# A two-layer graph network on one core: leaks taken from PSUM in groups of eight pairs, terms made a batch ahead

## The chip, the cores and the metric

The kernel runs on one core of a Trainium2 chip. A core has TensorE (PE, matrix products; PEld is its loading of weights), VectorE (DVE), ScalarE (ACT), GpSimd (POOL) and SyncE (SP). Each takes its instructions in order from its own queue, and semaphores join them. SP, ACT and POOL also start DMA transfers. SBUF is the working memory of 128 partitions, PSUM the smaller memory that TensorE writes into, in banks of 2 KB a partition, which is 512 numbers of four bytes. The metric is the time of one execution on the device in microseconds (us).

## The reference, cut to what matters

There are 12,500 nodes with 64 features and 400,000 edges, which are sorted by their target. The first layer computes a message per edge and sums the messages by target:

```
x_i, x_j = x[dst], x[src]
h = leaky_relu(concat([x_i, x_j - x_i]) @ W1 + b1, 0.01)
h = leaky_relu(h @ W2 + b2, 0.01)
x = layernorm(x + segment_sum(h, dst))
```

The second layer is an attention over the same edges and one loop per node, with four heads: logits `a_src[src] + a_dst[dst]`, a leak of 0.2, a softmax over the edges of a target, a weighted sum of the sources' features, the mean over the heads, and again a layernorm of the sum.

## The kernel before, in words

The first product is split: `x_i @ (W1a - W1b) + b1` belongs to the target and `x_j @ W1b` to the source, so both are computed once per node, and an edge needs one addition only. The nodes are ranked by their number of edges and cut into 98 windows of 128, one node to a partition. Window `w` has `KW[w]` edge slots, 64 in the first, 46 in the second, down to 19 in the last, 3180 in all. The kernel has three stages.

**Preparation** (L461 to L697). Nodes lie in 98 columns of 128. The columns go in eight batches: six of 14, then 8, then 6. For each batch POOL fetches a row of edge data per column (`gather_rows` into `rt`, L585). The class `Terms` makes the two products of four columns: `turn` transposes on TensorE and copies to `xt` on ACT; `multiply` forms `pab` on TensorE, then VectorE adds `b1` into `rt` (L499) and ACT copies twice into `bt` (L503, L504). The class `Bins` counts nodes by degree, four columns at a time: `mark` makes the one-hot `oh` on VectorE (L517), three sorts of small products on TensorE (L522, L526, L529) and a copy on ACT; `place` multiplies and reduces on VectorE (L535, L537). `in_step` sets the order of these in every queue: the terms of batch `k` go with the bins of batch `k - 1`. Behind each pass come `lt` and its reduction (L590, L593), which need the fetched rows of batch `k`, and from them the degrees, which the next bins need. SP writes `rt` and `info` to the table `xtab` and loads the node features of batch `k + 2` into one of three buffers `rt`. After the last pass the ranks follow (L610 to L697), and `bt` is written to the tables `btab`.

**First layer** (L834 to L990). `load_rows` fetches the rows of several windows from `xtab`, and `index_slots` turns them into indices on VectorE (`make_slots`, L253 to L265, and `mask_slots`). `fetch0(w)` lets POOL gather a row of 128 nodes for each slot, two slots side by side as a pair, into `g`, which has five buffers (`gp`). It is called two windows ahead. Pairs are worked on in groups of up to four: `expand` transposes each pair into PSUM (L878) and VectorE adds the target's term on the way to SBUF (L880); `leak` multiplies by 0.01 and takes the maximum, in place in SBUF (L884); `second` is the second product (L889), brought to SBUF by ACT with the bias (L891), and a leak again; `collect` sums over the pairs by a product with `both`, which TensorE accumulates in PSUM (L898), and VectorE reduces that at the window's end (L903). `norm` adds the node's own features, takes the layernorm and, from `g`, writes the sources' ranks over the indices; `logits` makes the attention terms and SP writes the rows to `t1tab` and `state`. The loop at L968 is an order written out by hand: in step `i` the second product of group `i - 2`, the expansion of group `i`, the collection of group `i - 4`, with norm and logits one and two steps behind. A window's groups come last pairs first, so that a window starts when most of its rows are there.

**Second layer** (L1058 to L1226). POOL gathers rows of `t1tab` for the same 3180 slots; VectorE weighs and reduces them (L1129, L1136). It needs the whole of `t1tab`, so that its first gather waits for the last window of the first layer.

Of the kernel before, what the change touches and what calls it, by code (L numbers as in the profile page):

```python
# [21 lines left out]
P = 128  # L22
# [40 lines left out]
def tile_gnn_resnorm(ctx: ExitStack, tc: tile.TileContext, x, src, dst, w1, b1, w2, b2,  # L63
# [397 lines left out]
    with tc.tile_pool(name="prep", bufs=1) as prep, \  # L461
            tc.tile_pool(name="prep2", bufs=2) as prep2, \
            tc.tile_pool(name="prep3", bufs=3) as prep3, \
# [17 lines left out]
        class Terms:  # L481
# [12 lines left out]
            def multiply(self):  # L494
                n, g0, g1 = self.n, self.g0, self.g1
                pab = pps2.tile([P, 4, 2 * D], F32, name="pab")
                for w in range(n):
                    nc.tensor.matmul(pab[:, w, :], self.xt[:, w, :], wab, start=True, stop=True)
                nc.vector.tensor_tensor(  # L499
# [39 lines left out]
        def load_inputs(b0, b1_):  # L539

            n = b1_ - b0
            rt = prep3.tile([P, DW, X0 + ER], F32, name="rt")
# [4 lines left out]
            for l0, l1 in ((0, cut), (cut, NFULL)):  # L547
                if l0 < l1:
                    nc.sync.dma_start(
                        rt[l0:l1, :n, :D],  # L550
                        x[l0 * NW:l1 * NW, :].rearrange("(p w) d -> p w d", w=NW)[:, b0:b1_, :])
            if b0 < NREST:
                c1 = min(b1_, NREST)
                nc.sync.dma_start(
# [4 lines left out]
        def degrees(a, b):  # L559
            nc.vector.tensor_sub(deg[:, a:b], ptr[:, a + 1:b + 1], ptr[:, a:b])  # L560
            nc.scalar.copy(info[:, a:b, 1], deg[:, a:b])
            nc.scalar.copy(info[:, a:b, 2], ptr[:, a:b])
            nc.sync.dma_start(xtab_v[:, a:b, XL:], info[:, a:b, :])
            return [Bins(g, min(g + 4, b)) for g in range(a, b, 4)]

        def in_step(terms, bins):
            for i in range(max(len(terms), len(bins)) + 1):
                if i < len(terms):
# [3 lines left out]
                if i < len(terms):  # L572
                    terms[i].multiply()
                if 0 <= i - 1 < len(bins):
                    bins[i - 1].place()

        rts = [load_inputs(*batches[0]), load_inputs(*batches[1])]
        nc.vector.tensor_sub(wab[:, :D], w1a, wab[:, D:])
        bins = []
        sorted_to = 0  # L580
        for k, (b0, b1_) in enumerate(batches):
# [4 lines left out]
            in_step([Terms(rt, b0, g, min(g + 4, b1_)) for g in range(b0, b1_, 4)], bins)  # L586
# [17 lines left out]
            if k + 2 < len(batches):  # L604
                rts.append(load_inputs(*batches[k + 2]))
# [95 lines left out]
    with tc.tile_pool(name="l0", bufs=1) as l0:  # L701
# [132 lines left out]
        with tc.tile_pool(name="m0", bufs=2) as mp, \  # L834
                tc.tile_pool(name="m0_t", bufs=4) as tp, \
                tc.tile_pool(name="m0_h", bufs=4) as hp, \
                tc.tile_pool(name="m0_x", bufs=3) as xp, \
                tc.tile_pool(name="m0_g", bufs=5) as gp, \
                tc.tile_pool(name="m0_ps", bufs=2, space=PSUM) as mps, \
                tc.manual_schedule():  # L840
            per = G // 2
            raws, own = {}, {}

            def fetch0(w):
                if w in batches:
                    index_slots(mp, *raws[w])
# [25 lines left out]
            def expand(q):  # L872
# [4 lines left out]
                for p in range(p0, p0 + n):  # L877
                    nc.tensor.transpose(q.pt[:, p - p0, :], g[:, p, 1:1 + 2 * D], ident)  # L878
# [375 lines left out]
```

## Time and profile before

| | us |
|---|---|
| median of three runs (8651.25 to 8656.24) | 8656.15 |
| the profiled execution | 8639.11 |
| its span, first to last instruction | 8637.4 |
| POOL busy in the span (74%) | 6381.8 |
| VectorE busy (49%) | 4242.0 |
| TensorE busy (21%) | 1855.1 |
| ACT busy (11%) | 953.0 |
| POOL's gathers of the first layer, 3180 at 969 ns | 3082.6 |
| POOL's gathers of the second layer, 3180 at 944 ns | 3002.9 |

How to read the profile: a row of the groups names the line of the kernel, the engine, the operation, the output and inputs by the program's names, the shape, and the number of instructions; then the busy time in us and the mean duration of one in ns; then the idle time of the engine just before these instructions, and what ended most of it. "issue" stands for time in which the engine waited for nothing that the profile shows. In the timeline a row begins with its start and duration in us, and brackets hold the idle time before it. In the table by stage a row has the stretch in us, its length, the busy time of PE, PEld, DVE, ACT and POOL with the number of instructions, the granted clock of TensorE, the share of the DMA engines' time and the GB/s. POOL is counted busy while it makes the transfers of a gather, not in the 0.3 us between two.

### The profile page before, as it was taken

To read this page: it belongs to the slowest core of one execution; us is meant where nothing else is said; L and a number is where in the kernel's file an instruction comes from. 1 tells how busy PE (TensorE), PEld (TensorE's weight loads), DVE (VectorE), ACT (ScalarE), POOL (GpSimd) and SP (SyncE) were. 2 spreads that over 40 slices of the span, in tenths; PEclk is the share of its full clock that TensorE was granted. 3 is DMA by queue.
4 is the path that set the end of the run, shared out by engine and by line. 5 is a ranking of instruction groups with operands and counts; after the bars stand their busy time and mean duration, and the time that the engine had idled before them with its cause. 6 is when DMAs were issued, how large, how long until landed. Compare 5 with 4: busy or idle time off the path is not lost. (4 is left out here: it accounts for less than half of the span.)

```text
span 8637.4 us, 30329 instructions
## 1 busy us (share of the span) xinstructions
PE 1855.1 (21%) x5401; PEld 816.5 (9%) x5402; DVE 4242.0 (49%) x6604; ACT 953.0 (11%) x2268; POOL 6381.8 (74%) x6668
## 2 busy tenths in 40 slices
PE   4233343433333333333430000000000000000000
PEld 3211111111111111111110000000000000000000
DVE  4432323323323332333325666666666666666667
ACT  2111010111111111111110000000000001101111
POOL 4477777777777777777767777777777777777776
PEclk9766665666666666666665555555555555555555
DMA  6211111111111111111112111111111111111111
GB/s 137 61 33 30 32 31 33 34 31 33 34 31 34 34 35 35 31 35 35 36 33 30 31 31 32 31 32 32 31 32 32 32 32 33 32 33 33 33 33 26
DMA packets 313179, 308.33 MB, mean 36 GB/s; under 512 B 164924, under 2 KB 204331, under 8 KB 312347
## 3 DMA queue, kind: packets, MB, share of 16 engines
q0 software_dynamic: 216064, 242.80, 14.9%
q1 hardware_dynamic: 96632, 61.87, 2.8%
q10 hardware_dynamic: 282, 1.63, 0.1%
q14 instruction: 154, 1.26, 0.0%
q8 instruction: 47, 0.77, 0.0%
HBM read 262.66 MB, written 43.18 MB: 35 GB/s over the span
## 5 line engine op out<-in xcount | busy, mean ns | idle before, releaser
L278 POOL DMA_INDIRECT g<-btab,idx_all x3180 | 3082.6, 969 | 976.0 <-issue 940.2
L278 POOL DMA_INDIRECT g<-t1tab,idx_all x3180 | 3002.9, 944 | 998.8 <-issue 923.8
L880 DVE TENSOR_TENSOR ht<-pt,at 128x512 f32<-128x512 f32 (+3 forms) x453 | 292.8, 646 | 2684.8 <-PE pt L878 2680.6
L1136 DVE TENSOR_REDUCE red<-wx 128x256 f32<-128x4096 f32 (+12 forms) x192 | 1389.3, 7236 | 0.1
L878 PE MATMUL pt<-ident,g 128*128 128x128 f32 x1663 | 404.5, 335 | 2608.2 <-DMA g<-btab,idx_all 2608.0
L1129 DVE TENSOR_TENSOR wx<-g,wt 128x4096 f32<-128x4096 f32 (+12 forms) x192 | 877.0, 4568 | 166.0 <-ACT wt L1108 166.0
L1158 PE MATMUL pn<-ident,nrm 128*128 128x128 f32 x196 | 67.3, 447 | 3911.7 <-DVE nrm L1154 3865.1
L1087 DVE TENSOR_TENSOR lg<-g,ad 128x128 f32<-128x128 f32 (+24 forms) x101 | 29.7, 294 | 1135.1 <-DMA g<-t1tab,idx_all 797.2
L889 PE MATMUL py<-ht,w 128*128 128x512 f32 (+3 forms) x906 | 578.4, 726 | 1.7 <-DVE ht L884 1.7
L898 PE MATMUL acc<-t,both 128*64 128x512 f32 (+3 forms) x906 | 571.6, 720 | 0.0
L878 PEld LDWEIGHTS pt<-ident,g 128*128 128x128 f32 x1663 | 253.1, 164 | 2987.9 <-issue 2852.6
L891 ACT ACTIVATE t<-py,b_col 128x512 f32<-128x512 f32 (+3 forms) x453 | 294.1, 649 | 1145.8 <-PE py L889 1143.8
L1158 PEld LDWEIGHTS pn<-ident,nrm 128*128 128x128 f32 x196 | 28.3, 203 | 3929.9 <-DVE nrm L1154 3709.2
L884 DVE SCALAR_TENSOR_TENSOR ht<-ht 128x512 f32<-128x512 f32 (+3 forms) x453 | 295.1, 651 | 15.5
L1090 ACT ACTIVATE lg_low<-lg 128x128 f32<-128x128 f32 (+24 forms) x101 | 27.8, 275 | 2435.5 <-DVE lg L1087 2435.5
L884 DVE SCALAR_TENSOR_TENSOR t<-t 128x512 f32<-128x512 f32 (+3 forms) x453 | 290.3, 641 | 1.0 <-ACT t L891 0.9
L889 PEld LDWEIGHTS py<-ht,w 128*128 128x128 f32 x906 | 169.1, 232 | 259.4 <-ACT t L891 74.7
L278 POOL DMA_INDIRECT xab<-xtab,node_i x98 | 97.8, 997 | 123.0 <-issue 120.0
L933 ACT COPY x1t<-px 64x128 f32<-64x128 f32 x98 | 25.3, 258 | 1298.2 <-PE px L931 1297.2
L278 POOL DMA_INDIRECT rt<-etab,first_i x98 | 99.8, 1018 | 89.3 <-SPq L400 43.2
L916 ACT ACTIVATE cn<-pz,npad 128x64 f32<-128x64 f32 x98 | 30.7, 313 | 1119.5 <-PE pz L909 1021.3
L283 POOL DMA_INDIRECT out_dram<-o,node_i x98 | 96.7, 987 | 60.0 <-issue 30.8
(209 smaller groups left out, 2686.8 us busy)
## 6 DMA issues: line engine op xcount, KB each, us to landing
g<-btab,idx_all POOLq DMA_INDIRECT x3180, 2.4
g<-t1tab,idx_all POOLq DMA_INDIRECT x3180, 2.4
state<-st SPq DMA_DIRECT2D x98, 134.0 KB
st<-state SPq DMA_DIRECT2D x98, 134.0 KB
xtab<-rt SPq DMA_DIRECT2D x6, 2016.0 KB
btab<-bt SPq DMA_DIRECT2D x2, 3185.0 KB
t1tab<-t SPq DMA_DIRECT2D x98, 34.0 KB
x<-t1tab SPq DMA_DIRECT2D x98, 32.0 KB
```

The lines of the kernel that those rows point to most:

```text
L278: nc.gpsimd.indirect_dma_start(out=o, out_offset=None, in_=table[:, :], in_offset=bass.IndirectOffsetOnAxis(ap=idx, axis=0))
L283: nc.gpsimd.indirect_dma_start(out=table[:, :], out_offset=bass.IndirectOffsetOnAxis(ap=idx, axis=0), in_=i, in_offset=None)
L878: nc.tensor.transpose(q.pt[:, p - p0, :], g[:, p, 1:1 + 2 * D], ident)
L880: nc.vector.tensor_tensor(q.h[:, :n, :], q.pt[:, :n, :], terms[q.w][:, None, :].to_broadcast([P, n, P]), op=ALU.add)
L884: nc.vector.scalar_tensor_tensor(x, x, 0.01, x, op0=ALU.mult, op1=ALU.max)
L889: nc.tensor.matmul(py[:, :n, :], w2_2, q.h[:, :n, :], start=True, stop=True)
L891: nc.scalar.activation(q.t[:, :n, :], py[:, :n, :], AF.Identity, bias=b2_col)
L898: nc.tensor.matmul(sums[q.w][:, :q.n, :], both, q.t[:, :q.n, :], start=q.first, stop=q.last)
L916: nc.scalar.mul(cn, pz[:, D:], npad)
L1129: nc.vector.tensor_tensor(f.wx[:, :n], f.g[:, j0:j0 + n, None, :D].to_broadcast([P, n, H, D]), f.wt[:, j0:j0 + n, :, None].to_broadcast([P ...
L1136: nc.vector.tensor_reduce(red.rearrange("p h d -> p (h d)"), f.wx[:, :n].rearrange("p k h d -> p (h d) k"), AX.X, ALU.add)
L1158: nc.tensor.transpose(pn[:, j, :], f.nrm[:, 2 * j:2 * j + 2, :], ident)
```

## The change

It has two parts that do not touch each other.

In the preparation the terms of batch 0 are made ahead of the loop, and pass `k` makes the terms of batch `k + 1` together with the bins of batch `k - 1`. `multiply` is cut in two: the product, and `store`, which holds the addition on VectorE and the two copies on ACT. In `in_step` the product of step `i - 1` stands ahead of the turn of step `i`, and its store behind the bins' mark and place. The buffers `rt` become four, the first three loads are issued ahead (two from ACT's queue, one from SP's), and the later ones three batches ahead. The copies to `info` and their write move from behind the degrees into the next pass.

In the first layer groups have up to eight pairs (two PSUM banks) instead of four, which makes 251 groups of the 453. A leak is no longer one instruction in SBUF: ACT writes 0.01 times the PSUM tile to SBUF and VectorE takes the maximum of the PSUM tile and that. The addition of the target's term stays in PSUM. The pairs' results of a window stand in `outs`, one buffer for the whole window, and are summed by one reduction on VectorE from SBUF instead of by products on TensorE. The gathered rows `g` have four buffers instead of five, the buffers of the index work one instead of two. The last window's groups come first pairs first, and the last four groups take their second product one step earlier.

```diff
-            tc.tile_pool(name="prep3", bufs=3) as prep3, \
+            tc.tile_pool(name="prep4", bufs=4) as prep4, \
...
             def multiply(self):
...
+                self.pab = pab
+
+            def store(self):
+                n, g0, g1, pab = self.n, self.g0, self.g1, self.pab
                 nc.vector.tensor_tensor(
...
         def in_step(terms, bins):
             for i in range(max(len(terms), len(bins)) + 1):
+                if 0 <= i - 1 < len(terms):
+                    terms[i - 1].multiply()
                 if i < len(terms):
                     terms[i].turn()
                 if i < len(bins):
                     bins[i].mark()
-                if i < len(terms):
-                    terms[i].multiply()
                 if 0 <= i - 1 < len(bins):
                     bins[i - 1].place()
+                if 0 <= i - 1 < len(terms):
+                    terms[i - 1].store()
+                if i == 0 and bins:
+                    store_info(bins[0].g0, bins[-1].g1)
...
-        rts = [load_inputs(*batches[0]), load_inputs(*batches[1])]
+        rts = [load_inputs(*batches[k], (nc.scalar, nc.scalar, nc.sync)[k]) for k in range(3)]
...
+        in_step(terms_of(0), [])
...
-            in_step([Terms(rt, b0, g, min(g + 4, b1_)) for g in range(b0, b1_, 4)], bins)
+            in_step(terms_of(k + 1), bins)
...
-            if k + 2 < len(batches):
-                rts.append(load_inputs(*batches[k + 2]))
+            if k + 3 < len(batches):
+                rts.append(load_inputs(*batches[k + 3], nc.sync))
...
-                tc.tile_pool(name="m0_h", bufs=4) as hp, \
+                tc.tile_pool(name="m0_h", bufs=2) as hp, \
+                tc.tile_pool(name="m0_l", bufs=1) as lp, \
+                tc.tile_pool(name="m0_s", bufs=1) as sp, \
+                tc.tile_pool(name="m0_y", bufs=2) as yp, \
...
-                tc.tile_pool(name="m0_g", bufs=5) as gp, \
+                tc.tile_pool(name="m0_g", bufs=4) as gp, \
...
+                nc.vector.tensor_tensor(q.pt[:, :n, :], q.pt[:, :n, :],
+                                        terms[q.w][:, None, :].to_broadcast([P, n, P]), op=ALU.add)
+                q.low = lp.tile([P, per, P], F32, name="low0")
+                nc.scalar.mul(q.low[:, :n, :], q.pt[:, :n, :], 0.01)
+
+            def leak(q):
+                n = q.n
                 q.h = hp.tile([P, per, P], F32, name="ht")
-                nc.vector.tensor_tensor(q.h[:, :n, :], q.pt[:, :n, :],
-                                        terms[q.w][:, None, :].to_broadcast([P, n, P]), op=ALU.add)
-
-            def leak(x):
-                nc.vector.scalar_tensor_tensor(x, x, 0.01, x, op0=ALU.mult, op1=ALU.max)
+                nc.vector.tensor_tensor(q.h[:, :n, :], q.pt[:, :n, :], q.low[:, :n, :], op=ALU.max)
 
             def second(q):
...
+                py = pyp.tile([P, per, P], F32, name="py0")
+                for p in range(0, n, BANK):
+                    m = min(BANK, n - p)
+                    nc.tensor.matmul(py[:, p:p + m, :], w2_2, q.h[:, p:p + m, :], start=True,
+                                     stop=True)
+                low = lp.tile([P, per, P], F32, name="low1")
+                nc.scalar.activation(low[:, :n, :], py[:, :n, :], AF.Identity, bias=b2_low,
+                                     scale=0.01)
+                nc.vector.scalar_tensor_tensor(outs[q.w][:, p0:p0 + n, :], py[:, :n, :], b2_col,
+                                               low[:, :n, :], op0=ALU.add, op1=ALU.max)
+
+            def collect(w):
+
+                n = KW[w] // 2 + 1
+                t = outs[w]
+                sums[w] = mp.tile([P, P], F32, name="ts")
+                nc.vector.tensor_reduce(sums[w], t[:, :n, :].rearrange("d j p -> d p j"), AX.X,
+                                        ALU.add)
...
+            at = [i + (2 if i < len(queue) - 4 else 1) for i in range(len(queue))]
+            for i in range(len(queue) + 3):
+                for f, w in late.pop(i, ()):
+                    f(w)
+                if 0 <= i - 1 < len(queue):
+                    leak(queue[i - 1])
+                now = [q for q, k in zip(queue, at) if k == i]
                 if i < len(queue):
                     q = queue[i]
-                    if q.first:
-                        if q.w + 2 < NW:
-                            bufs[q.w + 2] = fetch0(q.w + 2)
+                    if q.first and q.w + 2 < NW:
+                        bufs[q.w + 2] = fetch0(q.w + 2)
                     expand(q)
...
+                for q in now:
+                    second(q)
                     if q.last:
-                        late[i + 1] = (norm, q.w)
-                        late[i + 2] = (logits, q.w)
-                if i in late:
-                    late[i][0](late[i][1])
+                        collect(q.w)
+                        late.setdefault(i + 1, []).append((norm, q.w))
+                        late.setdefault(i + 2, []).append((logits, q.w))
```

## The prediction

> **What bounds the kernel now.** I read the table of groups first, then the stages by window, then the timeline around POOL's gaps.
>
> ```profile
> L278 POOL DMA_INDIRECT g<-btab,idx_all x3180 | 3082.6, 969 | 976.0 <-issue 940.2
> L278 POOL DMA_INDIRECT g<-t1tab,idx_all x3180 | 3002.9, 944 | 998.8 <-issue 923.8
> L880 DVE TENSOR_TENSOR ht<-pt,at 128x512 f32<-128x512 f32 (+3 forms) x453 | 292.8, 646 | 2684.8 <-PE pt L878 2680.6
> L1136 DVE TENSOR_REDUCE red<-wx 128x256 f32<-128x4096 f32 (+12 forms) x192 | 1389.3, 7236 | 0.1
> L884 DVE SCALAR_TENSOR_TENSOR ht<-ht 128x512 f32<-128x512 f32 (+3 forms) x453 | 295.1, 651 | 15.5
> L884 DVE SCALAR_TENSOR_TENSOR t<-t 128x512 f32<-128x512 f32 (+3 forms) x453 | 290.3, 641 | 1.0 <-ACT t L891 0.9
> ```
>
> POOL issues one gather per instruction, 0.94 us plus 0.31 us between two. 6360 of them at 1.25 us are 7950 of the 8637 us, and nothing else is near. A gather of the first layer takes 25 ns more than one of the second; 3180 x 25 ns = 80 us. The same views by stage (POOL is the last busy column, DMA share the last but one):
>
> ```profile
> 45.90:243.00 197.10, 102.98 (x520) 79.02 (x520) 105.64 (x184) 45.89 (x128) 99.76 (x98) 1.00 0.68 132
> 296.00:4471.30 4175.30, 1523.43 (x3926) 579.63 (x3926) 1316.94 (x3498) 471.90 (x1213) 3177.52 (x3275) 0.63 0.17 33
> 4471.30:4495.40 24.10, 14.65 (x39) 5.24 (x38) 12.70 (x49) 7.37 (x24) 0.04 (x1) 0.78 0.10 25
> 4495.40:8637.00 4141.60, 176.83 (x588) 119.35 (x588) 2750.72 (x2684) 388.60 (x796) 3099.58 (x3278) 0.50 0.16 32
> ```
>
> Four stages: preparation, where POOL is busy half the time; first layer, POOL without a gap; a hole of 24 us; second layer, POOL again. The change touches the first three.
>
> **Why the first layer's gathers are longer.** The timeline at one long gather:
>
> ```profile
> 448.67 0.69 DVE L880 TENSOR_TENSOR ht<-pt,at 128x512 f32<-128x512 f32 x1 [2.66 <-PE pt L878]
> 449.40 0.69 DVE L884 SCALAR_TENSOR_TENSOR ht<-ht 128x512 f32<-128x512 f32 x1
> 449.68 1.22 POOL L278 DMA_INDIRECT g<-btab,idx_all  x1 [0.31 <-issue]
> 450.00 0.68 DVE L884 SCALAR_TENSOR_TENSOR t<-t 128x512 f32<-128x512 f32 x1
> 451.21 0.94 POOL L278 DMA_INDIRECT g<-btab,idx_all  x1 [0.30 <-issue]
> ```
>
> The gather starts inside the leak of L884, which ends at 450.09; it takes 0.28 us too long, so it went on where the leak ended, as if it needed something of VectorE's some 0.13 us after its start. I did this for all 3275 gathers from 296 to 4495 us: what VectorE runs 135 ns after the start, and the time over the median of 944 ns:
> - L884's leaks, both tensor inputs in SBUF: 439 gathers, 269 of them over 20 ns long, 67.7 us in sum
> - L261, L263, L265 of the index work, both inputs in SBUF: 108 gathers, 82 long, 19.4 us
> - everything else (L880 with one input in PSUM: 174 gathers, none long; the reduction L903: 39, none) and idle: about -1 us.
>
> The second layer agrees: L1136 reads one SBUF tensor, L1129 and L1143 one SBUF and one PSUM tensor, all there run beside gathers, and its 3316 POOL instructions are 7 us over 944 ns in sum.
>
> **Leaks from PSUM.** The two leaks go. In their place, for 1663 pairs in 251 groups instead of 453: the addition now stays in PSUM, ACT makes 0.01 of it, a maximum takes one input from PSUM and one from SBUF; after the second product ACT again makes the low side and one VectorE instruction adds the bias and takes the maximum, PSUM and SBUF. None has two SBUF tensor inputs, so they stand with L880 and L1143: 0. The sum over pairs leaves TensorE (906 products of 720 ns, beside POOL, worth nothing) for one reduction per window from SBUF. By L1136 (6996 ns for 4096 elements) it takes 1.7 ns an element: 17 pairs, 2176 elements, 3.7 us a window, beside a window's 40 us of gathers (32 x 1.25). VectorE's busy share here is 1317 of 4175 us; 98 x 3.7 more is covered by POOL, and were the cover gone it would be those 363 us. Its pull on gathers: by L903 and L1136 0; if it held POOL as a leak does, the first gather to start in it would wait for the rest, 3.7 - 0.6 = 3.1 us, 98 times, 304 us. I take 0 and keep the 304 out of the range, since L1136 is the same operation from SBUF and lies beside gathers for 1047 us without lengthening one. So this part gives 67.7 us; the index work's 19 us stays and may fall anywhere from 8 to 30, since it depends on where the starts fall. Bounds 55 to 80.
>
> The Trainium skill speaks against this term. Its page "SBUF — State Buffer", section "Who interferes with whom", says that a VectorE instruction with two SBUF inputs contends only with a GpSimd instruction that reads SBUF, and infers that tensor_tensor leaves descriptor generation alone because that needs the write side. By that inference the leaks cost the gathers nothing, this term would be 0 and the sum 36 us; by the rows above, which show gathers held until a leak ends, it is 68 and the sum 104. I go by the rows.
>
> **Preparation.** POOL does not bind it. The rank work starts at 243.0 us (L610), POOL's last fetch ended at 191.9, and its 15.27 us wait at 184.64 is only for a buffer; from 243.0 it is 42.4 us to the first xab gather at 285.35, unchanged. What binds is the chain of 8 passes over TensorE, ACT and VectorE:
>
> ```profile
> 186.13 0.59 PE L522 MATMUL pr<-oh,upper_b 128*128 128x512 bf16 x1 [0.59 <-DVE oh L517]
> 189.27 0.69 DVE L499 TENSOR_TENSOR rt<-pab,b_bc 128x512 f32<-128x512 f32 x1 [3.19 <-PE pab L498]
> 189.88 0.68 DVE L535 TENSOR_TENSOR sel<-pr,oh 128x512 f32<-128x512 f32 x1
> 190.59 0.69 DVE L537 TENSOR_REDUCE rank<-sel 128x4 f32<-128x512 f32 x1
> 191.38 0.69 DVE L517 TENSOR_TENSOR oh<-key,col_k 128x512 bf16<-128x512 bf16 x1
> 192.13 0.59 PE L522 MATMUL pr<-oh,upper_b 128*128 128x512 bf16 x1 [1.91 <-DVE oh L517]
> 285.35 0.94 POOL L278 DMA_INDIRECT xab<-xtab,node_i  x1 [93.46 <-issue]
> ```
>
> TensorE waits 1.91 us for a one-hot that VectorE makes only after three other things. A pass of 14 columns, first L522 to first L522, takes 27.3 us (99.5, 126.9, 154.2, 181.5). In the new order the product of step i-1 stands before the turn of step i, and VectorE makes the one-hot before the store, so a step is TensorE's own: product 2.0, turn 1.06, marks 1.02, together 4.1 us. A pass: 1.0 + 2 x 4.1 + 3.3 (half step) + 1.2 + 0.5 (last store) = 14.2, and from lt to the next L522 5.9 (2.03 + 2.02 + 0.18 + 0.17, a memset of some 0.3, 0.15 + 0.69, gaps): 20.1. Walk: terms of batches 0 and 1 from 50.2, 14 us each (now 15.3; the copy to xt no longer stands behind the two to bt), 1 us for three loads at once: lt at 79; first L522 at 85.6; four passes and 1.8 for the weight terms, 167.8; the passes with 8 and 6 new columns 16.6 and 13.2, 197.6; 6.9 and 3.0 for the last two: 207.5 against 243.0, 35.5 us. Each lt comes 15 us or more after its batch has been gathered (17.5 us a batch from 46). The loads now wait in ACT's queue too: six issues of at most 0.9 us from 45.4 (SP's rows), done before ACT's first copy at 51. On SP the info writes move behind a later load; nobody reads them before 285. The fourth buffer removes the 15 us wait, worth nothing by itself. DMA has 134 us of share in 197 us, and would have it in 162: 0.83, some delay. I take 33; if steps cost 4.7 as the better ones do now and loads come late, 15; at best 38.
>
> **The hole at 4471.** From the last transposes at 4473.61 to the first t1tab gather at 4495.44 it is 21.8 us now. After: transposes 0.6, the second product of the group before 3.1 (it stands behind them in TensorE's order), its low side and maximum 2.0, state 0.5, leak 0.7, product 2.0, low and maximum 1.5, reduction of 10 pairs 2.2, transposes and three additions 1.4, from bn_stats on 5.4 as now (4490.07 to 4495.44): 19.4. Gain 3, between -3 and 8.
>
> **Sum.** 33 + 68 + 3 = 104 us. The profiled execution took 8639.1 (span 8637.4), which gives 8535; the median of the runs is 17.0 higher, and carried over 8656 - 104 = 8552. A measurement here tells about 0.2%, 17 us, from none.
>
> **Rivals.**
> - The preparation gains nothing, because the passes meet the DMA engines: 96 to 106 and 126 to 136 us show a share over 1.2 already. Against: averages of 0.68, and lt is 15 us behind its data. Then 68 + 3: 8585.
> - The leaks were not what lengthened the gathers, the change does not do its work there. For: 170 of the 439 that start under a leak are not long, and TensorE and ACT work at those moments too. Against: a leak that ends within 135 ns of the sampled moment costs little by itself, and no gather is long under L880, beside which they work as well. Then 33 + 3 = 36: 8620.
> - Slower: the gathered rows have four buffers instead of five, so window w+2 waits for the norm of w-2. If that norm ran only in the burst after w+1, POOL would stand for a burst, 11 us (4337.4 to 4348.6), in 94 windows: +1030, 9590. It decides from 1.1 us a window on. Against: a norm stands three steps after its window's last group, a window has at least two groups, so it is emitted before the fetch that needs the buffer, in the burst of w-1, some 80 us of gathers before w+2's turn.
>
> **Numbers.** Forecast 0.80, rivals 0.07, 0.05, 0.05, no net effect 0.03. The ends: 38 + 80 + 8 = 126 gives 8530, 15 + 55 - 3 = 67 gives 8589, which holds the first rival; I widen by 3. Faster 0.92, same 0.03, slower 0.05.
>
> **What would show it.** Mean of g<-btab near 950 ns, long only under L261 to L265's successors; rank work near 208 to 212 us; no POOL wait in the first layer; the hole at 19 us. I am wrong if the reduction or the maximum lengthens gathers, if a pass stays over 24 us, or if POOL waits for g.

## The result, and the profile after

The changed kernel took 8553.3 us (median of 4 runs, 8550.6 to 8554.2) against 8654.5 for the kernel before on the same chip. The ratio is 0.9883, with a 95% interval from 0.9866 to 0.9900. The forecast was 8552, within 8527 to 8592.

The table of groups of the changed kernel (busy us, mean ns of one, idle time before them):

```profile
L278 POOL DMA_INDIRECT g<-t1tab,idx_all x3180 | 3010.4, 947 | 1003.3 <-issue 924.2
L278 POOL DMA_INDIRECT g<-btab,idx_all x3180 | 3024.1, 951 | 976.6 <-issue 943.9
L1167 DVE TENSOR_REDUCE red<-wx 128x256 f32<-128x4096 f32 (+12 forms) x192 | 1389.2, 7236 | 0.1
L903 DVE TENSOR_TENSOR pt<-pt,at 128x1024 f32<-128x1024 f32 (+4 forms) x251 | 262.0, 1044 | 1747.3 <-PE pt L902 1747.2
L925 DVE SCALAR_TENSOR_TENSOR t<-py,b_col,low 128x1024 f32<-128x1024 f32 (+4 forms) x251 | 276.2, 1101 | 631.7 <-ACT low L923 631.6
L933 DVE TENSOR_REDUCE ts<-t 128x128 f32<-128x2176 f32 (+13 forms) x98 | 371.0, 3786 | 3.4
L911 DVE TENSOR_TENSOR ht<-pt,low 128x1024 f32<-128x1024 f32 (+4 forms) x251 | 259.1, 1032 | 1.5 <-ACT low L906 1.5
```

A gather of btab now takes 951 ns, 4 ns more than one of t1tab; before it was 25 ns. VectorE does more work than before in the first layer (1582 us of busy time against 1317; the reduction alone is 371), and the gathers are shorter all the same. The one surprise in these rows is t1tab: 947 ns here, 944 before, in a layer that the change does not touch.

The stages of the changed kernel by windows (start and end, length, busy us and count of PE, PEld, DVE, ACT and POOL, granted clock, DMA share, GB/s):

```profile
45.90:207.50 161.60, 101.44 (x520) 78.68 (x520) 106.34 (x184) 45.57 (x128) 99.61 (x98) 1.00 0.78 160
260.50:4372.80 4112.30, 1158.24 (x3134) 621.12 (x3134) 1581.69 (x3000) 556.66 (x1072) 3114.11 (x3275) 0.59 0.17 33
4372.80:4401.00 28.20, 9.61 (x24) 4.71 (x22) 14.54 (x37) 5.92 (x18) 0.03 (x1) 0.56 0.08 20
4401.00:8551.00 4150.00, 176.89 (x588) 119.43 (x588) 2750.54 (x2684) 388.73 (x796) 3107.41 (x3278) 0.50 0.16 32
```

The rank work starts at 207.5 us (243.0 before), the first layer is 63 us shorter, the gap between the layers 4 us longer, and the second layer 8 us longer. Together that is 86 us of span, where the medians differ by 101. The 15 us between the two come back below: they go with the 3 ns on every gather, which no later profile of this kernel has.

One step of the preparation in the changed kernel's timeline (start, length, engine, line, and in brackets the idle time before and what ended it):

```profile
152.34 1.06 PE L490 MATMUL pt<-ident,rt 128*64 128x128 f32 x4
152.44 0.69 DVE L503 TENSOR_TENSOR rt<-pab,b_bc 128x512 f32<-128x512 f32 x1 [1.06 <-PE pab L498]
...
153.19 0.63 PE L526 MATMUL pr<-oh,upper_b 128*128 128x512 bf16 x1
...
153.62 0.63 PE L530 MATMUL po<-ident_b,oh 128*128 128x128 bf16 x4
...
154.04 0.29 PE L533 MATMUL pbin<-ones_b,oh 128*128 128x1 bf16 x4
...
154.26 2.07 PE L498 MATMUL pab<-wab,xt 64*128 64x128 f32 x8
...
156.26 1.06 PE L490 MATMUL pt<-ident,rt 128*64 128x128 f32 x4
...
157.12 0.63 PE L526 MATMUL pr<-oh,upper_b 128*128 128x512 bf16 x1
```

TensorE goes from turn to marks to product to the next turn without a wait for VectorE, 3.9 us from one L526 to the next. Before, it stood for a one-hot 0.6 us in the second step of a pass and 1.9 to 2.1 us in the third and fourth. A pass of 14 columns takes 19.7 to 20.3 us instead of 27.3.

### The profile page after: what moved, and what is told of

Read it like the earlier page. It is cut to its first block, busy times and chain, and to the rows that moved or that the text cites. A ratio compares the mean times of both kernels' runs of the same rounds, so it can differ in the third digit from the quotient of the medians.

```text
span 8551.0 us, 28389 instructions
## 1 busy us (share of the span) xinstructions
PE 1483.3 (17%) x4593; PEld 857.0 (10%) x4594; DVE 4509.0 (53%) x6096; ACT 1036.0 (12%) x2121; POOL 6326.6 (74%) x6668
## 5 line engine op out<-in xcount | busy, mean ns | idle before, releaser
L278 POOL DMA_INDIRECT g<-btab,idx_all x3180 | 3024.1, 951 | 976.6 <-issue 943.9
L1167 DVE TENSOR_REDUCE red<-wx 128x256 f32<-128x4096 f32 (+12 forms) x192 | 1389.2, 7236 | 0.1
L903 DVE TENSOR_TENSOR pt<-pt,at 128x1024 f32<-128x1024 f32 (+4 forms) x251 | 262.0, 1044 | 1747.3 <-PE pt L902 1747.2
L902 PE MATMUL pt<-ident,g 128*128 128x128 f32 x1663 | 463.8, 401 | 2033.5 <-DMA g<-btab,idx_all 2032.2
L925 DVE SCALAR_TENSOR_TENSOR t<-py,b_col,low 128x1024 f32<-128x1024 f32 (+4 forms) x251 | 276.2, 1101 | 631.7 <-ACT low L923 631.6
L906 ACT ACTIVATE low<-pt 128x1024 f32<-128x1024 f32 (+4 forms) x251 | 220.3, 877 | 2681.8 <-DVE pt L903 2681.8
L902 PEld LDWEIGHTS pt<-ident,g 128*128 128x128 f32 x1663 | 302.7, 199 | 2185.5 <-issue 1961.5
L933 DVE TENSOR_REDUCE ts<-t 128x128 f32<-128x2176 f32 (+13 forms) x98 | 371.0, 3786 | 3.4
L1121 ACT ACTIVATE lg_low<-lg 128x128 f32<-128x128 f32 (+24 forms) x101 | 27.9, 276 | 2443.7 <-DVE lg L1118 2443.7
L920 PEld LDWEIGHTS py<-ht,w 128*128 128x128 f32 x906 | 236.5, 291 | 261.3 <-issue 172.9
L923 ACT ACTIVATE low<-py,b_low 128x1024 f32<-128x1024 f32 (+4 forms) x251 | 244.0, 972 | 138.9 <-PE py L920 138.6
L911 DVE TENSOR_TENSOR ht<-pt,low 128x1024 f32<-128x1024 f32 (+4 forms) x251 | 259.1, 1032 | 1.5 <-ACT low L906 1.5
L297 ACT ACTIVATE ln_sd<-ln_mv,eps_t 128x1 f32<-128x1 f32 x196 | 57.7, 294 | 1123.3 <-DVE ln_mv L295 1123.3
```

The source lines that it names most:

```text
L278: nc.gpsimd.indirect_dma_start(out=o, out_offset=None, in_=table[:, :], in_offset=bass.IndirectOffsetOnAxis(ap=idx, axis=0))
L903: nc.vector.tensor_tensor(q.pt[:, :n, :], q.pt[:, :n, :], terms[q.w][:, None, :].to_broadcast([P, n, P]), op=ALU.add)
L906: nc.scalar.mul(q.low[:, :n, :], q.pt[:, :n, :], 0.01)
L911: nc.vector.tensor_tensor(q.h[:, :n, :], q.pt[:, :n, :], q.low[:, :n, :], op=ALU.max)
L920: nc.tensor.matmul(py[:, p:p + m, :], w2_2, q.h[:, p:p + m, :], start=True, stop=True)
L923: nc.scalar.activation(low[:, :n, :], py[:, :n, :], AF.Identity, bias=b2_low, scale=0.01)
```

## The experiments

All kernels below ran beside runs of the kernel before on the same chip. Its median there was 8634.8 to 8637.6 us, some 18 us under that of the first comparison. So most of the times expected below count from 8655 or 8553 us and are to be read as differences. The excess of a gather is its duration less the median gather of its own execution.

### The two parts alone

The first kernel is the one before with the hunks of the diff up to the line `rts.append(load_inputs(...))`, the second the one before with the hunks of the first layer.

> The kernel before with the preparation of the changed kernel alone. Theory (the two parts add up): the rank work starts at 207 to 209 us as in the changed kernel, against 243.0; the first layer keeps its mean of 967 to 970 ns for a gather of btab and its hole of 24 us; the time is 35 us under the kernel before, 8619 (8612 to 8626). Rival (the gain of the preparation is lost again, because the gathers only start earlier against the same later work): the same rank work, and a time within 15 us of the kernel before.

> The kernel before with the first layer of the changed kernel alone. Theory: the rank work stays at 243 us, a gather of btab takes 949 to 953 ns, the hole is 27 to 29 us, and the time is 101 - 35 = 66 us under the kernel before, 8589 (8580 to 8597). Rival (the leaks were not what lengthened the gathers, and the shorter first layer came from the earlier start): 8640 to 8655.

Measured: the preparation alone 8601.0 us, ratio 0.9962 (0.9948 to 0.9976), 33.8 us under the kernel before; the first layer alone 8574.3 us, ratio 0.9930 (0.9911 to 0.9946), 60.6 us under it. The times themselves were missed by 15 to 18 us, since the kernel before took 8635 us here; the differences were expected as 35 and 66. By stages of the profiled executions:

| kernel | first btab gather | first layer | gap | second layer | span |
|---|---|---|---|---|---|
| before | 296.03 | 4175.3 | 24.10 | 4141.9 | 8637.4 |
| preparation alone | 261.02 | 4171.8 | 25.67 | 4142.3 | 8600.8 |
| first layer alone | 296.22 | 4106.6 | 27.92 | 4142.7 | 8573.5 |
| changed, first profile | 260.51 | 4112.3 | 28.19 | 4150.0 | 8551.0 |
| changed, profiled again | 260.51 | 4106.2 | 27.92 | 4142.1 | 8536.8 |

The spans fall by 36.6 and 63.9 us, 100.5 together; the changed kernel, profiled again, falls by 100.6. By the spans the parts add up. By the medians they are 33.8 + 60.6 = 94.4 us against 98.7 for the changed kernel (measured in a later series, below), some 4 us apart; the runs of the kernel before alone lie between 8631.6 and 8640.1, so that the medians don't tell whether a few us are given back. The rival to each part falls.

### What in the preparation did it

Two things changed there: the order within a step, and the terms made a batch ahead. Each was taken alone. Order only:

```
-        in_step(terms_of(0), [])
...
-            in_step(terms_of(k + 1), bins)
+            in_step(terms_of(k), bins)
```

> The changed kernel, but pass k makes the terms of batch k, as before the change, in the new order within a step. Theory (it is the order of the instructions of a step, the product of step i-1 before the turn of step i and the one-hot before the store, that shortens a pass): a pass of 14 columns takes 20 us, the rank work starts at 201 to 208 us, and the time is that of the changed kernel, 8547 to 8556. Rival (it is the terms made a batch ahead, which no longer wait for a batch that is just being fetched): the rank work at 225 us or later, 8570 or more.

Ahead only:

```
-                if 0 <= i - 1 < len(terms):
-                    terms[i - 1].multiply()
                 if i < len(terms):
                     terms[i].turn()
                 if i < len(bins):
                     bins[i].mark()
+                if i < len(terms):
+                    terms[i].multiply()
+                    terms[i].store()
                 if 0 <= i - 1 < len(bins):
                     bins[i - 1].place()
-                if 0 <= i - 1 < len(terms):
-                    terms[i - 1].store()
```

> The changed kernel with the terms made a batch ahead, but the old order within a step: product and store of a step right behind its marks, the placing of the step before behind them. Theory (the order within a step is what counts): a pass of 14 columns takes 26 to 28 us, the rank work starts at 238 to 252 us, the time is 8583 to 8600. Rival (the batch ahead is what counts): the rank work at 205 to 212 us and 8548 to 8558.

Measured: with the order only the rank work starts at 206.4 us and the time is 8537.3 us, 97.6 under the kernel before (the changed kernel on this chip: 98.7 under). With the batch ahead only the rank work starts at 246.2 us and the time is 8577.7, 57.1 under, about what the first layer alone gives. In the timeline of the second, TensorE stands again:

```profile
157.65 1.49 PE L498 MATMUL pab<-wab,xt 64*128 64x128 f32 x6
...
159.17 0.69 DVE L503 TENSOR_TENSOR rt<-pab,b_bc 128x512 f32<-128x512 f32 x1 [3.18 <-PE pab L498]
...
159.78 0.68 DVE L539 TENSOR_TENSOR sel<-pr,oh 128x512 f32<-128x512 f32 x1
...
160.49 0.69 DVE L541 TENSOR_REDUCE rank<-sel 128x4 f32<-128x512 f32 x1
161.10 0.15 DVE L518 SCALAR_TENSOR_TENSOR key<-deg,spare_k 128x2 bf16<-128x2 f32 x1
161.28 0.42 DVE L521 TENSOR_TENSOR oh<-key,col_k 128x256 bf16<-128x256 bf16 x1
161.76 0.37 PE L526 MATMUL pr<-oh,upper_b 128*128 128x256 bf16 x1 [2.06 <-DVE oh L521]
```

It waits 2.06 us for the one-hot that VectorE makes behind the store, the multiplication and the reduction, as in the kernel before. So the gain of the preparation comes with the order within a step. Making terms ahead gives nothing; without the new order the rank work even starts 3 us later than in the kernel before. Both kernels have the fourth buffer and the earlier loads: with the old order these bring nothing either. Whether the new order needs them was not run.

### Is it the two inputs in SBUF, or any work of VectorE?

One more instruction in each of the 251 groups of the changed kernel, in two forms of equal size. The first reads two tensors from SBUF, the second one from PSUM and one from SBUF:

```
                 nc.vector.tensor_tensor(q.h[:, :n, :], q.pt[:, :n, :], q.low[:, :n, :], op=ALU.max)
+                more = lp.tile([P, per, P], F32, name="more")
+                nc.vector.tensor_tensor(more[:, :n, :], q.h[:, :n, :], q.low[:, :n, :], op=ALU.max)
```

```
+                nc.vector.tensor_tensor(more[:, :n, :], q.pt[:, :n, :], q.low[:, :n, :], op=ALU.max)
```

> The changed kernel with one more maximum on VectorE in each of the 251 groups, of h and the low side, both in SBUF, 128 x up to 1024; nobody reads its output. Theory (a VectorE instruction with two SBUF tensor inputs holds a gather that starts under it until it ends): by the rule of the kernel before, a gather that starts s after the instruction is (its length - s - 0.13 us) too long; with starts spread evenly over 1.25 us and lengths of 0.65 to 1.27 us that is 93 us over 251 instructions (40 to 230, as the starts are not spread evenly), so the first layer takes about 4205 us against 4112 and the time is 8645 (8595 to 8785); only gathers that start under the new instruction are longer. Rival (any work of VectorE beside POOL costs this, or the loss comes from the time VectorE is busy): the same as the run with the instruction that reads PSUM and SBUF, whatever that is.

> The changed kernel with the same additional maximum in each group, but of pt in PSUM and the low side in SBUF; nobody reads its output. Theory: no gather is longer, mean of a btab gather 949 to 953 ns, and only the hole grows, by 1 to 3 us: 8550 to 8558. Rival (any further VectorE work beside POOL costs time): some 93 us more, as with two inputs in SBUF.

Measured: two inputs in SBUF 8621.6 us (8618.3 to 8623.2), one 8540.3 us (8539.0 to 8540.4), beside 8538.9 for the changed kernel on this chip. The new instruction is of the same length in both, 1044 and 1030 ns in the mean. The gathers of the kernel with two inputs in SBUF, in its table of groups:

```profile
L278 POOL DMA_INDIRECT g<-btab,idx_all x3180 | 3099.9, 975 | 976.1 <-issue 952.3
```

and of the kernel with one:

```profile
L278 POOL DMA_INDIRECT g<-btab,idx_all x3180 | 3019.3, 949 | 976.0 <-issue 951.7
```

975 against 949 ns. The same place in the timeline of each, first with two inputs in SBUF (L913 is the new instruction):

```profile
352.88 1.22 DVE L911 TENSOR_TENSOR ht<-pt,low 128x1024 f32<-128x1024 f32 x1
352.95 0.94 POOL L278 DMA_INDIRECT g<-btab,idx_all  x1 [0.30 <-issue]
...
354.12 1.22 DVE L913 TENSOR_TENSOR more<-ht,low 128x1024 f32<-128x1024 f32 x1
354.20 1.97 POOL L278 DMA_INDIRECT g<-btab,idx_all  x1 [0.30 <-issue]
355.27 1.22 DVE L903 TENSOR_TENSOR pt<-pt,at 128x1024 f32<-128x1024 f32 x1
356.48 0.94 POOL L278 DMA_INDIRECT g<-btab,idx_all  x1 [0.30 <-issue]
```

and with one:

```profile
352.77 1.22 DVE L911 TENSOR_TENSOR ht<-pt,low 128x1024 f32<-128x1024 f32 x1
353.90 1.22 DVE L913 TENSOR_TENSOR more<-pt,low 128x1024 f32<-128x1024 f32 x1
353.98 0.94 POOL L278 DMA_INDIRECT g<-btab,idx_all  x1 [0.31 <-issue]
355.23 0.94 POOL L278 DMA_INDIRECT g<-btab,idx_all  x1 [0.30 <-issue]
```

Both gathers start 0.08 us into the additional maximum. One takes 1.97 us, the other 0.94. The gather that starts 0.07 us into L911 in the first of the two, a maximum of the same length from PSUM, takes 0.94 us as well.

Sorted by when a gather starts after the start of L913, in both traces:

| start after L913's start | two inputs in SBUF: gathers | rule: rest of L913 less 127 ns | measured excess | one input: gathers | measured excess |
|---|---|---|---|---|---|
| 0 to 50 ns | 12 | 951 | 0 | 3 | 2 |
| 50 to 300 ns | 49 | 701 | 701 | 64 | 0 |
| 300 to 600 ns | 73 | 483 | 483 | 58 | -1 |
| 600 to 900 ns | 44 | 244 | 244 | 40 | 0 |
| 900 to 1300 ns | 42 | 45 | 45 | 34 | -1 |

In sum the new instruction costs 82 us with two inputs in SBUF (93 expected) and 0 with one. The theory stands, and the rival falls: VectorE's work as such costs POOL nothing. The rule, with the starts as they fell, gives 94 us; the 11 us that are missing are the 12 gathers of the first row, which were not held at all. There it is the other way round: each of the 12 instructions under which they start takes 36 to 62 ns longer than the median one of its size, as if the gather went first and VectorE waited. With one input in SBUF none of the 251 is over 8 ns longer.

### Does the size of the groups matter?

```
-            per = 2 * BANK
+            per = BANK
```

> The changed kernel with groups of four pairs instead of eight: the same operands, some 1.8 times the instructions of a group. Theory (only where the operands lie matters, not the size of a group): a btab gather takes 949 to 953 ns, VectorE is busy some 40 us longer beside POOL, the gap at the end of the layer is 25 to 29 us, the time 8549 to 8558. Rival (fewer and larger instructions are part of the gain): a btab gather over 955 ns and a time over 8565.

Measured: 8542.1 us (8540.2 to 8542.8), 93.3 under the kernel before where the changed kernel is 98.7 under. A gather of btab takes 950 ns, VectorE is busy 4580 us against 4506 (74 us more, where 40 were expected), the first layer takes 4107.8 against 4106.2 us, and the gap 30.1 against 27.9 (25 to 29 expected). Four pairs give nearly all of it; eight are worth 3 us by the medians themselves and 5 by the differences to the kernel before, with 2 us in the gap and 2 in the layer. What counts is where the operands lie.

### The gap between the layers

It was forecast to shrink by 3 us, and grew by 4. The end of the first layer in the changed kernel's timeline, first profile:

```profile
4371.84 0.94 POOL L278 DMA_INDIRECT g<-btab,idx_all  x1 [0.30 <-issue]
...
4375.27 2.51 DVE L933 TENSOR_REDUCE ts<-t 128x128 f32<-128x1408 f32 x1
...
4377.83 0.47 PE L940 MATMUL pz<-ident,ts 128*128 128x128 f32 x1 [3.20 <-DVE ts L933]
...
4378.31 1.06 PE L902 MATMUL pt<-ident,g 128*128 128x128 f32 x4
...
4380.86 0.95 DVE L911 TENSOR_TENSOR ht<-pt,low 128x768 f32<-128x768 f32 x1
...
4381.96 2.90 PE L920 MATMUL py<-ht,w 128*128 128x512 f32 x4 [2.58 <-DVE ht L911]
...
4387.23 0.68 DVE L911 TENSOR_TENSOR ht<-pt,low 128x512 f32<-128x512 f32 x1
...
4391.65 2.30 DVE L933 TENSOR_REDUCE ts<-t 128x128 f32<-128x1280 f32 x1
...
4400.97 0.94 POOL L278 DMA_INDIRECT g<-t1tab,idx_all  x1 [28.19 <-DMA t1tab<-t]
```

The last gather ends at 4372.78, but the last transposes (L902) start only 5.5 us later, since they stand behind those of norm(96) on TensorE, and these wait for the reduction of window 96. Two kernels put other orders there. The first moves norms and logits of the last two steps behind the groups' work:

```
+                if not end <= i <= end + 2:
+                    for f, w in due:
+                        f(w)
...
+                if i == end + 1:
+                    for q in now:
+                        second(q)
+                    for f, w in due:
+                        if f is norm:
+                            f(w)
...
+                if end <= i <= end + 1:
+                    for f, w in due:
+                        if i == end or f is logits:
+                            f(w)
```

> The changed kernel, with the norms and logits of the last two steps behind the groups' own work: the last transposes no longer stand behind the transposes of norm(96), which wait for the reduction of window 96. Theory: the last transposes run within 3 us of the last gather's end (4372.78 plus its landing; 5.5 us now), the product of the group before lies ahead of them, and POOL's gap at the end of the first layer is 18 to 22 us against 28.2; the time is 6 to 10 us less, 8543 to 8548. Rival (the gap is the length of the chain from the last gather's landing whatever the order): the gap stays at 26 to 29 us, 8552 to 8556.

The second catches up earlier and puts a group's second product ahead of the next group's transposes:

```
-            at = [i + (2 if i < len(queue) - 4 else 1) for i in range(len(queue))]
+            at = [i + (2 if i < len(queue) - 8 else 1) for i in range(len(queue))]
...
+                if i >= end:
+                    finish(now, i)
...
                     expand(q)
...
+                if i < end:
+                    finish(now, i)
```

> The changed kernel with another order at the end of the first layer alone: the second products catch up eight groups before the end instead of four, and in the last two steps the second product, its leak and the reduction of a window stand ahead of the next group's transposes. Theory (the gap was long because VectorE's and TensorE's own orders put unfinished work of windows 95 and 96 ahead of the last group): the last transposes run within 2.5 us of the last gather's end, the last leak (L911) is done within 6 us of it, POOL's gap is 17 to 20 us against 28 to 29, the time 8 to 12 us under the changed kernel. Rival (the work of the last windows does not fit between the gathers however it is ordered, as the first attempt at the end suggests): a gap of 26 us or more, within 3 us of the changed kernel.

Both missed. The first took 8538.4 us with a gap of 29.2 us, the second 8541.5 with 29.8; the changed kernel on this chip 8538.9 with 27.9. The last transposes start later than before, not sooner: 8.0 and 12.4 us after the last gather's end, against 5.3. From the last leak (L911) to the first gather of t1tab it is 13.7 us in the changed kernel, 14.3 and 13.8 in the two others, so what differs lies ahead of that leak. The eight profiles that have the changed kernel's order at the end show gaps from 27.0 to 28.8 us, so that both other orders are 0.4 to 1 us above all of these and gain nothing. Ahead of the leak VectorE and TensorE work off windows 95 and 96, and each move seems only to have changed which piece came first. The cause can be narrowed down but was not settled: all windows but the last are worked through from their highest pairs, so window 96 cannot begin before its last gathers have landed (4347.8 in the second kernel's trace, where its first four transposes each wait for a gather), and its work and window 97's first group have only the 21 us until the last gather's end to hide in. Working the last windows in rising order would test it; it wasn't tried.

### The rest of the long gathers

In the changed kernel some 17 us of excess remain, nearly all of it under the index work of lines L261 to L265, three instructions over seven windows. They were cut to two per window:

```
-            nc.vector.tensor_tensor(dif, cur[:, :, s:s + width], cur[:, :, 0:width],
-                                    op=ALU.subtract)
-            nc.vector.tensor_tensor(dif, dif, bit[:, :, None].to_broadcast([P, nw, width]),
-                                    op=ALU.mult)
-            nc.vector.tensor_tensor(dif, dif, cur[:, :, 0:width], op=ALU.add)
+            for w in range(nw):
+                nc.vector.tensor_tensor(dif[:, w, :], cur[:, w, s:s + width], cur[:, w, 0:width],
+                                        op=ALU.subtract)
+                nc.vector.scalar_tensor_tensor(dif[:, w, :], dif[:, w, :], bit[:, w:w + 1],
+                                               cur[:, w, 0:width], op0=ALU.mult, op1=ALU.add)
```

> The changed kernel with the index work's three instructions over seven windows (lines L261 to L265, both tensor inputs in SBUF, 0.38 to 1.1 us) replaced by two per window of 0.1 to 0.2 us, the same result. Theory (a gather is held from 0.13 us after its start until the end of a VectorE instruction with two SBUF inputs, so an instruction hardly longer than that cannot hold one for long): the time of btab gathers over the median falls from 13 to 18 us to 0 to 4 us although there are more such instructions, and the time is 9 to 16 us under the changed kernel. Rival (it is the amount of two-input work that costs, however it is cut): over the median 13 us or more, a time within 4 us of the changed kernel.

The changed kernel itself ran in the same call:

> The changed kernel as it is, beside the variants that follow and on their chip. In the runs so far the median gather took 944 ns in every kernel, before the change and after, where the changed kernel's first profile had 947. Theory (the 3 ns belong to that execution's chip and not to the change): 944 ns here, a btab gather 949 ns in the mean, the second layer 4142 us, the time 101 us under the kernel before on the same chip, 8534 (8528 to 8540). Rival (the change makes every gather 3 ns longer): 947 ns, the second layer 4150 us, 8545 or more.

Measured: the changed kernel 8538.9 us (8537.4 to 8540.0), ratio 0.9886 (0.9870 to 0.9903); with the short instructions 8520.9 us (8520.6 to 8523.5), ratio 0.9866 (0.9850 to 0.9883). That is 17.9 us less, somewhat more than expected, and the two sets of runs lie 14 us apart. In the changed kernel the gathers are back at 944 ns and the second layer at 4142.1 us, so the rival to that run, that the change makes every gather 3 ns longer, falls. The gathers of the changed kernel here:

```profile
L278 POOL DMA_INDIRECT g<-btab,idx_all x3180 | 3018.6, 949 | 976.1 <-issue 952.1 <-DMA g<-btab,idx_all 14.0 <-DVE left L249 7.3
L278 POOL DMA_INDIRECT g<-t1tab,idx_all x3180 | 3002.9, 944 | 1002.7 <-issue 940.6 <-DMA g<-t1tab,idx_all 34.2 <-DMA t1tab<-t 27.9
```

and of the kernel with the short instructions:

```profile
L278 POOL DMA_INDIRECT g<-t1tab,idx_all x3180 | 3003.4, 944 | 1001.7 <-issue 945.2 <-DMA g<-t1tab,idx_all 29.6 <-DMA t1tab<-t 27.0
L278 POOL DMA_INDIRECT g<-btab,idx_all x3180 | 3002.4, 944 | 975.2 <-issue 950.5 <-DMA g<-btab,idx_all 14.9 <-DVE left L249 6.4
L264 DVE SCALAR_TENSOR_TENSOR dif<-dif,bit,dif 128x38 f32<-128x38 f32 (+37 forms) x588 | 156.3, 266 | 20.8
L262 DVE TENSOR_TENSOR dif<-dif 128x38 f32<-128x38 f32 (+37 forms) x588 | 115.9, 197 | 0.0
```

A gather of btab now takes what one of t1tab takes, 944 ns. The excess fell from 16.7 to 0.5 us, although VectorE is busy 130 us longer (4636 against 4506) and the index work reads two SBUF tensors in 1372 instructions and 329 us instead of 336 instructions and 161 us. It is the length of each that costs, not their number or sum; the rival falls.

### All together

Short index instructions, the second order of the end, and the terms of batch k in pass k:

> The short instructions of the index work, the second order at the end of the first layer, and the terms of batch k made in pass k. Theory (they add up): the rank work at 205 to 207 us, the gap at the end of the first layer 17 to 20 us, the excess of btab gathers 0 to 4 us, the time 20 to 28 us under the changed kernel, 8507 (8500 to 8516). Rival (gains at the seams are given back by a later wait): less than 12 us.

Measured: 8521.5 us (8520.6 to 8524.5), ratio 0.9867 (0.9851 to 0.9884), the same as with the short instructions alone. The 20 to 28 us under the changed kernel were missed (17.4), since the gap did not shrink: the rank work starts at 204.9 us, 3 us sooner than with the short instructions alone, and the gap is 30.1 us, 3 us longer. So none of the kernels that ran is faster than the changed one with the short index instructions; short instructions and the terms of batch k in pass k, with the end as in the changed kernel, weren't run together.

## Why the prediction was right, and where it was not

**What bounds.** POOL's gathers did bind, in every kernel here: the spans differ by what the gathers of the first layer, the preparation and the gap differ, and where a gather takes 944 ns the second layer lies between 4141.9 and 4142.8 us.

**Leaks from PSUM.** The step gave 67.7 us, with the index work's 19 us left over. With all gathers at 944 ns (the changed kernel profiled again against the kernel before) the first layer is 69.1 us shorter, and the excess of all its gathers fell from 86.0 to 16.8 us. The reduction and the new maximum were costed at nothing and cost nothing: none of the 291 gathers that start under the reduction in the run with one input in SBUF is over 17 ns too long. The end of 304 us that was kept out of the range was rightly kept out. One reading was off without harm: the second layer of the kernel before has 3278 POOL instructions, 5 us over 944 ns in sum, not 3316 and 7.

The rule that spoke against this step was put as the Trainium skill's, page "SBUF — State Buffer", section "Who interferes with whom": a VectorE instruction with two SBUF inputs contends with a GpSimd instruction that reads SBUF, and by inference, as descriptor generation needs the write side, tensor_tensor leaves that alone. The first half agrees with the runs (82 us with two inputs in SBUF, 0 with one), the inference does not carry over to these gathers: the instructions that were held are indirect gathers, one per 128 rows, and tensor_tensor holds them. That they are held because they read their indices from SBUF would fit both the 127 ns and the few instructions that wait for a gather instead, but no run separates it.

**Preparation.** Taken as 33 us, with a walk that gave 207.5 for the start of the rank work; it started at 207.47 and 207.50, a gain of 35.5. A pass was worked out as 20.1 us and takes 19.7 to 20.3; the first lt stood at 79 and came at 80.6, and each step is 3.9 instead of 4.1 us. The rival that the DMA engines bind falls. What the walk did not say, and the runs show, is that the order within a step gives all of this without the terms made ahead.

**The hole.** This is the term that failed: forecast 3 us of gain, measured a loss of 3.8 to 4.1, outside its bounds of -3 to 8. The transposes that it started from are not the last ones of the kernel before:

```profile
4473.61 0.48 PE L878 MATMUL pt<-ident,g 128*128 128x128 f32 x2
...
4476.05 0.60 PE L878 MATMUL pt<-ident,g 128*128 128x128 f32 x4
...
4495.44 0.94 POOL L278 DMA_INDIRECT g<-t1tab,idx_all  x1 [24.10 <-DMA t1tab<-t]
```

Those at 4473.61 turn the two pairs that were fetched last, and the window's last group follows at 4476.05. In the changed kernel the pairs fetched last are the last group, so the comparison is still one of like with like. The step counted 19.4 us from these transposes to the first t1tab gather and let them start as soon after the last gather as before (2.3 us). They start 5.3 to 5.5 us after it, behind the reduction and the transposes of window 96, and then it takes 22.6 us. Of the 3.3 us by which the 19.4 fell short, 3.1 lie between the transposes and the product of the group before: the sum lets the product follow after 0.6 us, and it follows after 3.65 (4378.31 to 4381.96), because it waits for the leak of its own group, and on VectorE that leak stands behind the norm of window 96 (from 4378.56 in the first profile). The sum has neither. The later start and the longer chain, 3.0 to 3.2 and 3.2 to 3.3 us, make up the 6.2 to 6.5 us between the 2.4 us less that the step worked out and the 3.8 to 4.1 us more that came.

**Sum and offset.** 104 us were forecast, 33 + 68 + 3; at an equal gather it is 35.5 + 69.1 - 3.8 = 100.8, and the spans give 100.6. The medians give 101.2 and 98.7. The offset of 17 us between the profiled execution and the median was carried over as it stood. It now has a likely reason: in the changed kernel's first profile the median gather takes 947 ns, and POOL is busy 13.9 us longer than in its second (6326.6 against 6312.7), with a span 14.2 us longer. No later profile has that, of this or another kernel, and beside them the kernel before took 8635 to 8638 us in the median, as in its profile, and not 8655. That its runs of 8655 us had 947 ns too wasn't traced. So the hit within 1.3 us owes something to errors that cancel: 7 us too much for the hole, 4 too little for the other two, and a start from 8656.2, the median of three runs, where a fourth makes it 8654.5.

**Rivals.** The first two fall with the parts run alone. In the third, POOL would stand for the buffer of the gathered rows; in the first profile no gap between two gathers of the first layer is over 0.4 us.

## What to carry to other kernels

Where POOL issues indirect gathers back to back, look at every VectorE instruction that reads two tensors from SBUF beside them: move one input to PSUM, or cut the instruction into pieces of 0.2 to 0.3 us, even if VectorE gets more work. In a loop of steps on several engines first look at who waits for whom within a step; a batch of work made ahead is worth nothing where the order of the step is what binds. And at the end of a stage count not only the last group's chain but all that stands ahead of it in each engine's order.

## What the runs showed of the hardware

- A gather that starts 59 ns or more after the additional VectorE instruction with two SBUF inputs is too long by that instruction's rest less 127 ns, to within 13 ns in each of 208 cases and within 1 ns in 126. One that starts in its first 31 ns isn't held (12 of 12), and then the instruction is 36 to 62 ns longer. Between 31 and 59 ns no gather started there; under the leaks of the kernel before, some that start 30 to 50 ns after are held and some are not.
- Short instructions can hold little, and where they do, it is by this rule. Of the gathers that start 50 to 100 ns after a short index instruction (73 of them, 0.25 us long in the mean) the rule gives 53 ns each, and 5 were measured. The two kinds differ. Take the gathers with 20 ns or more to lose by the rule: under the subtraction (L262) 16 of the 17 that start 25 ns or more after it are held as the rule says; under the product and sum (L264) none of the 52 that start in its first 100 ns is held, and all 9 that start later are. An L264 with a gather that starts 61 to 100 ns after it is 33 to 68 ns longer itself. Why a gather goes first for so much longer there, no run tells.
- The gather's own length differs from one series of runs to another, and not by kernel: 947 ns in the changed kernel's first profile, 944 in the profile of the kernel before and in all twelve kernels run afterwards, while VectorE's reduction (L1136 before, L1167 after) took 7236 ns in both first profiles. For a kernel of 6500 such instructions the two profiles of the changed kernel are 14 us or 0.2% apart, as much as some changes are worth, so that only runs made side by side should be compared.
